# A graph layer's opening: first-hop products in pairs over three slots, the first guess in one piece, list pieces counted anew

## The chip, the cores and the metric

The kernel runs on one core of one Trainium2 chip. The metric is device time in microseconds of one execution, the median of several runs; smaller is better. The profile is one further execution, with its own time.

## The reference

What is computed, cut to what matters (N = 3327 nodes, D = 256, d_attn = 64):

```
h  = relu(layernorm(x))
R  = adj + eye(N);  R = R / R.sum(-1)          # adj is sparse: some five entries a row
Xf = Xa = h;  Z = 0
for n in range(2):
    q = Xa @ W1.T @ W2.T;  k = Xa @ W3.T
    P = softmax(q @ k.T)
    A = P with only the largest entries of each row that make up 0.9 of it
    A = A / A.sum(-1)
    Xf = R @ Xf;  Xa = A @ Xa
    Z += Xf @ U1[n].T + Xa @ U2[n].T
out = x + layernorm(h + Z) * ln_g + ln_b
```

## The kernel before, in words

Rows are cut into NT = 26 tiles of 128. Two steps (n = 0, 1) follow each other, and each walks over the tiles in **slots**: in slot i (from -1 to 27) different tiles are at different stages. The functions named here are generators; each `next` runs them to their next `yield`.

**Stages of a tile in a step.** `weights` (L579) makes the tile's queries, the logits in four chunks (`pl`, two PSUM buffers of two banks in the pool `ps_l`), and their exponentials `e` on ACT. `measured` (L632 in step 0) guesses the threshold of the 0.9 mass: a head of small ACT steps (L617 to L639) and POOL steps (L640 to L643), two passes of ACT over the 3328 entries of each row (relu, then sign; L630), and a tail of small ACT steps (L650 to L656), which ends in five small DVE steps (L659 to L663). `settle` (L719) finds the exact threshold on DVE: `w` (L725, one instruction over 128x3328), 20 MAX8 over segments (`cand`, L730, in two halves), five rounds on the candidates (`bb`, L737 to L749), then the mask of `e` (L759, or in two pieces at L756 for the first and last tile). `Sums` (L792) transposes the masked `e` on PE (`pt`, L805), copies it on ACT (`eT`, L807) and multiplies it with the rows (`pa`, L819). `spread` (L1067) is the sparse product with R: `diffuse` (L902) multiplies gathered adjacency rows `ac` with gathered feature rows `xg` into `pr` (L905). `first_end` (L913) ends a tile of step 0 and, by `prep` (L478), writes next step's keys into the tile `after` and queries into `both`.

**The lists.** `listed` (L832) finds the nonzero columns of each row tile of adj. It loads the tile in pieces and takes the largest of each 128x128 block (`fm`, L841, DVE). The first HALVES = 9 tiles come in two pieces of 832 KB into four spare areas (`roomy`: the scan tile `w`, here called `wide`, and `es[2]`); later tiles come in seven pieces of up to 256 KB into `at` (two buffers). A list ends with some eight small DVE steps (L844 to L852). `packed` and `gathered` (L857, L869) turn a list into indices, load the diagonal block of adj (L883, SP), and issue ten indirect DMAs on POOL: five of adj rows (L888) and five of feature rows (L897), in step 0 from the DRAM table `bx`.

**The products.** Row tile t of h times both matrices of U1 (512 columns) is needed in two DRAM tables before the gathers: `ax[t]` (the part for the end) and `bx[:, t]` (the part to be spread). `products` (L976) makes them: two matmuls into one PSUM bank (`pz`, L982), taken in turn from `ps_r` and `ps_a`, one buffer each; then one copy (L985) into `uh`, four buffers in `es[3]`, on DVE or on ACT; then two DMA writes on SP (L986, L987). A table row that is gathered must have been written, so the first gather of `bx` waits for all 26 tiles.

**What sets the order.** On PE, ACT and DVE the instructions of the two steps stand in the order of the text (L1182 to L1185). That order is written by hand: each slot has seven parts, and a string for each part tells which generators are advanced, one letter for one `next`: m measured, d settle, s spread, w weights, e first_end, a a list piece, p packed, g gathered, b products, q the next tile's queries. `PLAN[0]` is step 0's (L1096). Beside it, two b come at the start of each part in slots -1 and 0 (L1158), and `work` (L1125 to L1138) bounds what a slot may take: list pieces are 3 in slot 0 and otherwise up to 9, of which five letters make five; products are MADE = 13 in slot -1 and the rest in slot 0 (L1152). At the slot's end what is left of the letters at L1174 is run out. POOL in step 0 and SP aren't tied to the text; a scheduler places them, and on each the instructions then run in that fixed order.

**The opening** (L997 to L1054) comes ahead of the slots: a loop over q = 0 to 17 takes pairs of row tiles through the layer norm (bn on DVE, `mv` in two buffers; rstd and scale on POOL, L1010 to L1013; relu on ACT, L1034), transposes (`pt`, L1036), keys and queries (`pk`, L1023; copied to `both` by DVE, L1000) and a Gram matrix (`pgram`, L1041). From q = 5 on one list piece is run in each turn (L1015). Two product tiles are started early by the scheduler, in this loop. After it `moments` (L501) turns the Gram matrix into what the guesses need (`gs`, `qm`), and `project` (L513) makes the first three tiles' laws (`mq`, L529 and L535; `ms` on POOL).

The lines that set the order, as they stand:

```
COUNTED = [t for t in range(NT - 2) if t % 2 == 0]
MADE = 13
HALVES = 9
...
    PLAN = (("mdsssa", "mcdsssa", "edawwp", "msda", "mpdea", "gdwwq", "emgq"),
...
                a=itertools.islice(lister, 9 if i else 3) if step == 0 else none,
...
                for c in "bb" + ({**OPEN, **LAST}.get(i, PLAN[1]) if step else PLAN[0])[k]:
                    next(work[c], None)
```

Of the kernel before, what the change touches and what calls it, by code (L numbers as in the profile page):

```python
# [9 lines left out]
F32 = mybir.dt.float32  # L10
# [8 lines left out]
P = 128  # L19
N = 3327  # L20
D = 256
DA = 64
NT = (N + P - 1) // P
NP = NT * P
ND = D // P
# [298 lines left out]
HALF = NT // 2  # L324
PARTS = -(-NT // 4)
AHEAD = (2, 2)
COUNTED = [t for t in range(NT - 2) if t % 2 == 0]
MADE = 13
HALVES = 9
FIRST = 8 * P  # L330
CUT = 4

# [12 lines left out]
def guess_graph_layer(ctx, tc, x, adj, w1t, w2t, w3t, u1t, u2t, ln_g, ln_b, out, flag):  # L345
    nc = tc.nc
# [8 lines left out]
    small = ctx.enter_context(tc.tile_pool(name="small", bufs=4))  # L355
    ps_l = ctx.enter_context(tc.tile_pool(name="ps_l", bufs=2, space=PSUM))
    ps_t = ctx.enter_context(tc.tile_pool(name="ps_t", bufs=2, space=PSUM))
    ps_a = ctx.enter_context(tc.tile_pool(name="ps_a", bufs=1, space=PSUM))
    ps_r = ctx.enter_context(tc.tile_pool(name="ps_r", bufs=1, space=PSUM))

    V, G, S, PE = nc.vector, nc.gpsimd, nc.scalar, nc.tensor

    rows_of = lambda t: min(P, N - t * P)
    valid = lambda t: 0 <= t < NT
# [8 lines left out]
    after = nodes.tile([P, HALF, P], F32, tag="after", name="after")  # L373
# [24 lines left out]
    u1 = const.tile([P, ND, 2, D], F32, tag="u1", name="u1")  # L398
# [1 line left out]
    gam = const.tile([P, D], F32, tag="gam", name="gam")  # L400
    bet = const.tile([P, D], F32, tag="bet", name="bet")
    uh = es[3][:, : 4 * (2 * D + 1)].rearrange("p (n d) -> p n d", n=4)
    G.memset(uh[:, :, 2 * D :], 1.0)
    for e in (es[0], es[1], es[3]):
        G.memset(e[:, N:NP], 0.0)
    half = const.tile([P, 4], F32, tag="half", name="half")
# [31 lines left out]
    ax = dram.tile([NT, P, D], F32, tag="ax", name="ax")  # L438
    bx = dram.tile([P, NT, D + 1], F32, tag="bx", name="bx")
# [5 lines left out]
    bb = const.tile([P, TOPK + 1], F32, tag="bb", name="bb")  # L445
# [505 lines left out]
    def proof():  # L951
        prove(1)
        yield
        pf = ps_t.tile([P, 4, P], F32, tag="pt", name="pf")
        PE.matmul(pf[:1, 0, :1], fl, ones, start=True, stop=True)
        V.tensor_copy(flag, pf[:1, 0, :1])

    live, ohs, acs, xgs, done, early = {}, {}, {}, {}, [], {}
    none = iter(())
# [14 lines left out]
    hT = xw.rearrange("p t (c r) -> p t c r", r=P)  # L974

    def products():  # L976

        for t in range(NT):
            pool, tag = ((ps_r, "pr"), (ps_a, "pa"))[t % 2]
            pz = pool.tile([P, 2 * D], F32, tag=tag, name="pz")  # L980
            for c in range(ND):
                PE.matmul(pz, hT[:, t, c, :], u1[:, c].rearrange("p n d -> p (n d)"),  # L982
                          start=c == 0, stop=c == ND - 1)
            u = uh[:, t % 4, :]
            (V.tensor_copy if t < MADE and t % 2 or t >= MADE and t % 3 == 0 else S.copy)(u[:, : 2 * D], pz)  # L985
            nc.sync.dma_start(ax[t], u[:, :D])  # L986
            nc.sync.dma_start(bx[:, t, :], u[:, D:])  # L987
            yield

    wide = scan.tile([P, NP], F32, tag="w", name="wide")  # L990
# [2 lines left out]
    lister, product = listed(), products()  # L993
# [3 lines left out]
    for q in range(HALF + 5):  # L997
        if 0 <= q - 3 < HALF:
            k, pk = q - 3, made.pop(q - 3)
            V.tensor_copy(both[:, :, k, :], pk[:, :2, :])  # L1000
            if 2 * k in COUNTED:
                V.tensor_copy(krs[:, k % 2, :DA], pk[:, 2, :DA])
        if q < HALF:
            mv = small.tile([P, 2, 2], F32, tag="mv2", name="mv2", bufs=2)
            rn = small.tile([P, 2, 2], F32, tag="rn2", name="rn2", bufs=3)
            for h in range(2):
                st = small.tile([P, 6], F32, tag="bn", name="st")
                V.bn_stats(st, x0[:, 2 * q + h, :])
                V.bn_aggr(mv[:, h, :], st)
            G.tensor_scalar(rn[:, 0, :], mv[:, :, 1], LN_EPS, None, ALU.add)  # L1010
            G.tensor_tensor(rn[:, 0, :], rn[:, 0, :], half[:, 0::3], ALU.pow)
            G.tensor_tensor(rn[:, 1, :], mv[:, :, 0], rn[:, 0, :], ALU.mult)
            G.tensor_scalar(rn[:, 1, :], rn[:, 1, :], -1.0, None, ALU.mult)  # L1013
            scaled[q] = rn
        if q >= 5:  # L1015
            run(lister, 1)
        if 0 <= q - 2 < HALF:
            k, pt = q - 2, turned.pop(q - 2)
            S.copy(hT[:, 2 * k : 2 * k + 2].rearrange("p t c r -> p (t c) r"), pt)
            pk = ps_t.tile([P, 4, P], F32, tag="pt", name="pk")  # L1020
            for h in range(2):
                for c in range(ND):
                    PE.matmul(pk[:, h, :], wk[:, c, h * DA : h * DA + P], hT[:, 2 * k + h, c, :],  # L1023
                              start=c == 0, stop=c == ND - 1)
            if 2 * k in COUNTED:
                for c in range(ND):
                    PE.matmul(pk[:, 2, :DA], hT[:, 2 * k, c, :], wk[:, c, :DA], start=c == 0, stop=c == ND - 1)
            made[k] = pk
        if 0 <= q - 1 < HALF:
            k, rn = q - 1, scaled.pop(q - 1)  # L1030
            pt = ps_t.tile([P, 4, P], F32, tag="pt", name="pt")
            for h in range(2):
                t = 2 * k + h
                S.activation(x0[:, t, :], x0[:, t, :], AF.Relu, bias=rn[:, 1, h : h + 1], scale=rn[:, 0, h : h + 1])  # L1034
                for c in range(ND):
                    PE.transpose(pt[:, 2 * h + c, :], x0[:, t, c * P : (c + 1) * P], ident)  # L1036
            turned[k] = pt
        if 0 <= q - 4 < HALF and 2 * (q - 4) in COUNTED:
            k = q - 4
            kr = krs[:, k % 2, :]  # L1040
            PE.matmul(pgram[:DA, : DA + 1], kr[:, :DA], kr, start=2 * k == COUNTED[0], stop=2 * k == COUNTED[-1])  # L1041
        if q == 6:
            run(begun[0], 1)
        if q in (8, 11, 14):
            run(begun[0], 1)
        if q in (9, 12):
            run(begun[q // 3 - 2], 1)
        if q == 5:
            for n in range(2):
                nc.sync.dma_start(u1[:, :, n], u1t[n].rearrange("(c p) e -> p c e", p=P))  # L1050
        if q == 10:
            pw = ps_t.tile([P, 4, P], F32, tag="pt", name="pw")
            PE.transpose(pw[:, 0, :], w2d, ident)
            S.copy(w2x, pw[:, 0, :])  # L1054
# [31 lines left out]
    def refetch(t):  # L1086
# [6 lines left out]

    PLAN = (("mdsssa", "mcdsssa", "edawwp", "msda", "mpdea", "gdwwq", "emgq"),  # L1096
            ("llcmss", "lnms", "lwwnfd", "lcmdsssggggg", "fsmwqdf", "llmdf", "lmwd"))

    LAST = {NT - 1: ("cfss", "cn", "nd", "sss", "fdddddsf", "f", ""), NT: ("c", "", "", "ff", "ff", "fv", "f"),
            NT + 1: ("fv", "f", "", "", "f", "f", "f")}  # L1100
    OPEN = {-1: ("llcmss", "lnms", "lwwnfd", "lcmdsssggggg", "fmgswqdf", "llmdf", "lmwfdm"),
            0: ("cmssggg", "nms", "wwnfd", "cmdsss", "fsmgwqdf", "mdf", "mwd"),
            1: ("cmss", "nms", "wwnfd", "cmdsssggggg", "fsmwqdf", "mgdf", "mwd")}
    OPEN[2] = OPEN[3] = OPEN[1]
    fetching = itertools.chain(*(refetch(t) for t in range(NT)))
# [6 lines left out]
    for step in range(2):  # L1112
        sums = Sums(step, live, xw if step else x0, AHEAD[step])

        for i in range(-1, NT + 2):
# [4 lines left out]
            if step == 1 and i == -1:  # L1120
# [9 lines left out]
                s=spread(step, i - 2 + 2 * step) if valid(i - 2 + 2 * step) else none,  # L1130
                w=later.pop((step, i + 2), none),
                e=first_end(i - 2) if step == 0 and valid(i - 2) else none,
                a=itertools.islice(lister, 9 if i else 3) if step == 0 else none,
                p=packed(i + 1) if step == 0 and i >= 0 and valid(i + 1) else none,
                g=fetching if step else gathered(i) if valid(i) else none,
                b=none, q=none, v=proof() if step and i == NT else work.get("v", none),
                l=laws(range(3, NT)) if step and i == -1 else work["l"] if step and i == 0 else none,
            )  # L1138
            if i >= 0 and valid(i + 3):
# [8 lines left out]
                work["w"] = begun[1] if step == 0 else itertools.chain(begun[1], begun[2])  # L1148
            if step == 0 and i == 0:
                work["w"] = begun[2]  # L1150
            if step == 0 and i < 1:
                work["b"] = itertools.islice(product, MADE if i else NT)  # L1152
            for k in range(PARTS):
                g = PARTS * (i - 1) + k - LATE[step]
                summing = valid(g // PARTS)
                if step and valid((g + AHEAD[1]) // PARTS):
                    sums.turn(g + (k == 2), min(i, NT - 1))
                for c in "bb" + ({**OPEN, **LAST}.get(i, PLAN[1]) if step else PLAN[0])[k]:  # L1158
                    next(work[c], None)
                if summing and not step:  # L1160
                    sums.turn(g, min(i, NT - 1))
                for n in BLOCKS[step].get(k, (0,)) if summing else ():
                    ended = sums.sum(g + n)
                    if ended and step == 0:
                        live["r", ended[0]] = ended[1]
                    elif ended:
                        work["f"] = finish(ended[0], live.pop(("f", ended[0])), *ended[1])
# [3 lines left out]
                G.memset(es[2][:, N:NP], 0.0)  # L1171
            if step and i < 1:
                next(fetching)
            for c in ("lcnwqsepb" if i > -1 else "cnwqsepb") if step else "cmwqsepgb":  # L1174
                run(work[c])
            if step == 0 and i == NT:
                moments(1, gsum)
# [52 lines left out]
```

## Time and profile before

| | |
|---|---|
| median of 3 runs | 1404.44 us (1404.25 to 1408.04) |
| the profiled execution: its time | 1405.77 us |
| its span, first to last instruction | 1404.0 us |
| granted TensorE clock, mean | 0.981 |
| end of the loop over q | 53.6 us |
| first w (L725) of step 0: tiles 0, 1, 2 | 86.04, 115.92, 141.07 us |
| later distances from w to w in step 0 | 23.8 to 26.6 us |
| first `pr` of a spread in step 0 | 143.35 us |

How to read it: the page gives for each engine the busy time and share (PE is TensorE's matmuls, PEld its weight loads, DVE VectorE, ACT ScalarE, POOL GpSimd, SP the engine that issues most DMAs; L and a number is a line of the kernel). A row of digits gives busy tenths in 40 equal slices of the span. In a list of waits stand the waiting engine and line, what released it, the total in us, how often, and the longest. In a timeline stand start, length, engine, line, operation, output and input with shapes, count, and in brackets the idle time ahead of it and what ended it. An fp32 matmul shows as two records.

### The profile page before, as it was taken

Reading aid. Unit: us, or ns where it says so; the run is one execution under the profiler, and the core shown is the slowest. Engines: PE = TensorE matmul, PEld = TensorE weight load, DVE = VectorE, ACT = ScalarE, POOL = GpSimd, SP = SyncE. Lnnn points to the kernel's source line nnn. Section 1 sums busy time; section 2 is a strip of 40 time slices with the busy share of each in tenths; the row PEclk is TensorE's granted clock in tenths of the full one; section 3 lists DMA queues with packets and bytes.
Section 4 is the critical chain, followed back from the end, with each engine's and each line's share of the span. In section 5 each row is a group of like instructions: output and inputs, shape, how many; then the busy total and the mean of one; then the engine's idle time right before and its main releaser. Section 6 shows DMA issues by size and latency. Waiting matters only on the chain.

```text
span 1404.0 us, 22095 instructions
## 1 busy us (share of the span) xinstructions
PE 1275.7 (91%) x6495; PEld 976.9 (70%) x6495; DVE 1195.0 (85%) x3673; ACT 1105.3 (79%) x2451; POOL 795.3 (57%) x1243
## 2 busy tenths in 40 slices
PE   6897999999999999999999759999999999999985
PEld 5545777777767777777777537777777777777764
DVE  6878898898988979989882489999998999999993
ACT  5467777878877778778773689999998999999941
POOL 6225766666657656666673475655655555565522
PEclk9999999999999999999999879999999999999998
DMA  8884453444444534534422121322312223132200
GB/s 279 269 269 122 118 145 109 128 138 117 128 125 115 143 107 122 146 111 125 126 78 83 51 72 45 90 77 60 91 56 80 67 70 88 50 89 73 63 20 22
DMA packets 91203, 149.77 MB, mean 107 GB/s; under 512 B 15266, under 2 KB 58657, under 8 KB 91073
## 3 DMA queue, kind: packets, MB, share of 16 engines
q1 hardware_dynamic: 73616, 105.37, 23.8%
q0 software_dynamic: 16640, 42.69, 12.3%
q8 instruction: 54, 0.88, 0.3%
q14 instruction: 77, 0.62, 0.1%
q10 hardware_dynamic: 816, 0.20, 0.1%
HBM read 120.93 MB, written 27.28 MB: 106 GB/s over the span
## 4 chain that ended last, share of the span: by engine, by line
PE 43%; DVE 40%; ACT 11%; issue 4%; DMA 1%; POOL 1%; SPq 0%; another core or an unknown queue 0%; DVEq 0%; ACTq 0%; POOLq 0%
PE pa L819 18%; DVE cand L730 8%; DVE w L725 7%; PE pt L805 6%; DVE e L759 5%; PE pr L905 4%; PE pl L597 4%; DVE cand L739 3%; ACT ja L630 3%; DVE bb L737 3%; PE pz L982 3%; PE pz L918 3%; DVE x L759 2%; ACT eT L807 2%; PE pk L1023 1%
## 5 line engine op out<-in xcount | busy, mean ns | idle before, releaser
L819 PE MATMUL pa<-xw,eT 128*128 128x256 f32 x1352 | 323.6, 384 | 27.4 <-DVE s L929 26.2
L630 ACT ACTIVATE ja<-e,g 128x3328 uint8<-128x3328 f32 x106 | 325.7, 3073 | 0.1
L819 PE MATMUL pa<-x,eT 128*128 128x256 f32 x1352 | 325.2, 382 | 0.0
L819 PEld LDWEIGHTS pa<-xw,eT 128*128 128x128 f32 x1352 | 250.7, 190 | 77.9 <-DVE s L929 31.6
L807 ACT COPY eT<-pt 128x512 f32<-128x512 f32 (+1 forms) x364 | 200.6, 559 | 119.8 <-PE pt L805 100.5
L819 PEld LDWEIGHTS pa<-x,eT 128*128 128x128 f32 x1352 | 244.8, 192 | 26.3
L730 DVE MAX8 cand<-w 128x8 f32<-128x168 f32 (+1 forms) x1040 | 251.4, 317 | 0.0
L805 PE MATMUL pt<-ident,e 128*128 128x128 f32 x1144 | 176.1, 276 | 18.2 <-DVE e L756 9.1
L897 POOL DMA_INDIRECT xg<-bx,index x130 | 156.6, 1205 | 45.2 <-issue 31.5
L805 PEld LDWEIGHTS pt<-ident,e 128*128 128x128 f32 x1144 | 140.9, 144 | 57.7 <-issue 29.2
L725 DVE SCALAR_TENSOR_TENSOR w<-e,g 128x3328 f32<-128x3328 f32 x44 | 162.1, 3684 | 0.7
L888 POOL DMA_INDIRECT ac<-in_adj,index x130 | 130.3, 1002 | 44.5 <-issue 29.6
L897 POOL DMA_INDIRECT xg<-vx,index x130 | 129.5, 996 | 38.6 <-issue 38.6
L759 DVE SCALAR_TENSOR_TENSOR e<-e,rec 128x3328 f32<-128x3328 f32 x40 | 147.5, 3688 | 0.6
L905 PE MATMUL pr<-xg,ac 128*128 128x257 f32 (+1 forms) x520 | 140.6, 395 | 6.8 <-DVE s L1080 6.8
L601 ACT ACTIVATE e<-pl 128x832 f32<-128x832 f32 x132 | 113.8, 867 | 17.9 <-PE pl L597 14.4
L905 PEld LDWEIGHTS pr<-xg,ac 128*128 128x128 f32 x520 | 94.0, 194 | 32.1 <-issue 14.2
L737 DVE MAX8 bb<-cand 128x8 f32<-128x160 f32 x286 | 92.6, 324 | 6.4
L597 PE MATMUL pl<-after,qT 64*128 64x416 f32 x416 | 95.5, 553 | 0.0
L597 PE MATMUL pl<-both,qT 64*128 64x416 f32 x416 | 90.4, 538 | 0.8 <-DVE both L1000 0.8
L673 POOL TENSOR_SCALAR g<-g,law 128x1 f32<-128x1 f32 x23 | 46.4, 2017 | 67.4 <-ACT g L672 67.4
L922 POOL TENSOR_TENSOR sv<-sv,x 128x256 f32<-128x256 f32 x26 | 19.8, 763 | 109.9 <-ACT sv L921 109.9
(255 smaller groups left out, 2153.5 us busy)
## 6 DMA issues: line engine op xcount, KB each, us to landing
at<-in_adj SPq DMA_DIRECT2D x102, 256.0 KB
cx<-ac SPq DMA_DIRECT2D x26, 384.0 KB
ac<-cx SPq DMA_DIRECT2D x26, 384.0 KB
wide<-in_adj SPq DMA_DIRECT2D x10, 832.0 KB
e<-in_adj SPq DMA_DIRECT2D x8, 832.0 KB
bx<-e SPq DMA_DIRECT2D x26, 128.5 KB
own<-bx SPq DMA_DIRECT2D x26, 128.5 KB
x<-in_x SPq DMA_DIRECT2D x13, 256.0 KB
```

Source lines behind the costliest of these rows:

```text
L597: PE.matmul(pl[:, a, :wd], qT[p, :], keys_of(step, a).rearrange("p a b -> p (a b)")[:, c : c + wd], start=True, stop=True)
L630: S.activation(ja, e, f, bias=guess, scale=sign, accum_out=total)
L725: V.scalar_tensor_tensor(w, e, col(16), e, ALU.is_lt, ALU.mult, accum_out=d2)
L730: V.max(cand[:, 8 * s : 8 * s + 8], w[:, s * SEG : min(NP, (s + 1) * SEG)])
L737: V.max(b8, cand)
L759: V.scalar_tensor_tensor(e, e, at(1), e, ALU.is_ge, ALU.mult, accum_out=ra)
L805: PE.transpose(pt[:, j, :], e[:, (j0 + j) * P : (j0 + j + 1) * P], ident)
L807: S.copy(eT[:, :w, :], pt[:, :w, :])
L819: PE.matmul(self.pa, eT[:, c - 4 * k, :], self.xa[:, j, :], start=c == 0, stop=c == NT - 1)
L888: G.indirect_dma_start(out=ac[:, k, :], out_offset=None, in_=rows, in_offset=bass.IndirectOffsetOnAxis(ap=index[:, t, k : k + 1], axis=0), ...
L897: G.indirect_dma_start(out=xg[:, k, :w], out_offset=None, in_=rows, in_offset=bass.IndirectOffsetOnAxis(ap=index[:, t, k : k + 1], axis=0))
L905: PE.matmul(pr[:, :w], ac[:, k, :], own if k == KT - 1 else xg[:, k, :w], start=k == 0, stop=k == KT - 1)
```

## The change

- `products` works on 13 pairs of tiles. Even pairs go into the two banks of `ps_r` and `ps_a`; odd pairs, and the last, into one two-bank buffer of the pool `ps_l`, which the logits use too. A pair takes two letters b: one for its four matmuls, one for its two copies and four writes. Copies are DVE's for the first four pairs and for odd ones, else ACT's.
- The copies of the last four tiles go into `uk`, three buffers in the tile `after`.
- Slots -1, 0 and 1 of step 0 get strings of their own (`BEGIN`), with 7, 12 and 7 letters b: 8, 12 and 6 tiles are multiplied in them. The two b ahead of each part go. In slot -1 relu and sign passes of tile 0's guess are advanced in one part, and the chunks of tile 1's logits come in parts 2 and 3 (before: 2 and 5).
- The gathers of tile 0 are begun in slot 0 and run out in part 3 of slot 1, after the last b.
- Lists: HALVES is 7, so 14 pieces are big and 133 small (18 and 119 before). The loop over q runs 10 pieces instead of 13; slots -1 and 0 run 4 and 6 (before 5 and 3), slot 1 and later odd slots 6, even ones 5 (before 5 each); part 5 of `PLAN[0]` gets the sixth a.
- `mv` has four buffers instead of two.

```diff
-MADE = 13
-HALVES = 9
+HALVES = 7
...
-    G.memset(uh[:, :, 2 * D :], 1.0)
+    uk = after.rearrange("p j r -> p (j r)")[:, : 3 * (2 * D + 1)].rearrange("p (n d) -> p n d", n=3)
+    for u in (uh, uk):
+        G.memset(u[:, :, 2 * D :], 1.0)
...
-        for t in range(NT):
-            pool, tag = ((ps_r, "pr"), (ps_a, "pa"))[t % 2]
-            pz = pool.tile([P, 2 * D], F32, tag=tag, name="pz")
-            for c in range(ND):
-                PE.matmul(pz, hT[:, t, c, :], u1[:, c].rearrange("p n d -> p (n d)"),
-                          start=c == 0, stop=c == ND - 1)
-            u = uh[:, t % 4, :]
-            (V.tensor_copy if t < MADE and t % 2 or t >= MADE and t % 3 == 0 else S.copy)(u[:, : 2 * D], pz)
-            nc.sync.dma_start(ax[t], u[:, :D])
-            nc.sync.dma_start(bx[:, t, :], u[:, D:])
+        for s in range(HALF):
+            if s % 2 or s == HALF - 1:
+                pl = ps_l.tile([P, 2, 512], F32, tag="pl", name="pz")
+                pzs = [pl[:, h, :] for h in range(2)]
+            else:
+                pzs = [ps_r.tile([P, 2 * D], F32, tag="pr", name="pz"), ps_a.tile([P, 2 * D], F32, tag="pa", name="pz")]
+            for h in range(2):
+                for c in range(ND):
+                    PE.matmul(pzs[h], hT[:, 2 * s + h, c, :], u1[:, c].rearrange("p n d -> p (n d)"),
+                              start=c == 0, stop=c == ND - 1)
+            yield
+            for h, pz in enumerate(pzs):
+                t = 2 * s + h
+                u = uh[:, t % 4, :] if t < NT - 4 else uk[:, t % 3, :]
+                (V.tensor_copy if s < 4 or s % 2 else S.copy)(u[:, : 2 * D], pz)
+                nc.sync.dma_start(ax[t], u[:, :D])
+                nc.sync.dma_start(bx[:, t, :], u[:, D:])
             yield
...
-            mv = small.tile([P, 2, 2], F32, tag="mv2", name="mv2", bufs=2)
+            mv = small.tile([P, 2, 2], F32, tag="mv2", name="mv2", bufs=4)
...
-        if q >= 5:
+        if 5 <= q < 15:
             run(lister, 1)
...
-    PLAN = (("mdsssa", "mcdsssa", "edawwp", "msda", "mpdea", "gdwwq", "emgq"),
+    PLAN = (("mdsssa", "mcdsssa", "edawwp", "msda", "mpdea", "gdawwq", "emgq"),
...
+    BEGIN = {-1: ("mba", "mmbba", "mwwbbaa", "bmwwb", "", "", ""),
+             0: ("mdbba", "mcdbba", "medbwwbap", "mdabb", "mpdbwwba", "gdabbq", "q"),
+             1: ("mdsssbba", "mcdsssbba", "edbawwbp", "msdbga", "mpdea", "dawwq", "emgq")}
...
-                a=itertools.islice(lister, 9 if i else 3) if step == 0 else none,
+                a=itertools.islice(lister, 5 + i % 2 if i > 0 else 6) if step == 0 else none,
...
-                g=fetching if step else gathered(i) if valid(i) else none,
-                b=none, q=none, v=proof() if step and i == NT else work.get("v", none),
+                g=fetching if step else itertools.chain(work.get("g", none), gathered(i)) if valid(i) else none,
+                b=none if step else product, q=none, v=proof() if step and i == NT else work.get("v", none),
...
-            if step == 0 and i < 1:
-                work["b"] = itertools.islice(product, MADE if i else NT)
...
-                for c in "bb" + ({**OPEN, **LAST}.get(i, PLAN[1]) if step else PLAN[0])[k]:
+                for c in ({**OPEN, **LAST} if step else BEGIN).get(i, PLAN[step])[k]:
...
-            for c in ("lcnwqsepb" if i > -1 else "cnwqsepb") if step else "cmwqsepgb":
+            for c in ("lcnwqsepb" if i > -1 else "cnwqsepb") if step else "cmwqsep" + "gb" * (i > 0):
```

## The prediction

> **What bounds the kernel now.** First the page: PE is the busiest engine and the chain that ended last is 43% PE, 40% DVE. The row of 40 slices (35.1 us each) shows where PE is not full in the first half: at the very start, and in the second (35 to 70 us, 8) and fourth (105 to 140, 7).
>
> ```profile
> PE 1275.7 (91%) x6495; PEld 976.9 (70%) x6495; DVE 1195.0 (85%) x3673; ACT 1105.3 (79%) x2451; POOL 795.3 (57%) x1243
> ...
> PE   6897999999999999999999759999999999999985
> ```
>
> The change lies wholly in the opening and slots -1 to 2 of step 0, with list pieces up to slot 23. So I cut that stretch by the busy time of the engines. Columns: length, then PE, PEld, DVE, ACT, POOL busy, granted clock, DMA share, GB/s.
>
> ```profile
> 17.17:53.60 36.43, 36.06 (x231) 28.59 (x231) 28.95 (x79) 17.40 (x36) 13.33 (x34) 1.00 0.84 287
> ...
> 114.00:119.30 5.30, 1.04 (x9) 0.80 (x7) 5.16 (x14) 4.90 (x12) 2.85 (x2) 1.00 0.14 50
> 119.30:126.10 6.80, 5.12 (x14) 3.79 (x16) 6.73 (x28) 2.69 (x5) 5.32 (x12) 0.50 0.40 128
> ```
> ```profile
> 53.60:143.35 89.75, 75.60 (x259) 39.82 (x257) 72.92 (x211) 59.26 (x139) 37.02 (x60) 0.96 0.64 200
> ```
>
> The loop over q runs at PE's speed (36.06 of 36.43). From its end to 143.35, where PE meets the first spread matmul `pr` of tile 0, PE idles 89.75 - 75.60 = 14.15 us, and 5.12 us of its work falls at half clock, which costs 2.6. So 16.7 us are to be had there, no more. Who holds PE:
>
> ```profile
> PE pt L805 <- ACT eT L807: 5.9, 1, 5.9
> PE pz L982 <- ACT e L985: 2.6, 1, 2.6
> PE po L873 <- ACT eT L807: 1.4, 1, 1.4
> PE pz L982 <- DVE e L985: 1.4, 1, 1.4
> PE pq L506 <- DVE lists L847: 1.1, 1, 1.1
> ```
>
> The longest is slot 1's start: PE's products are used up, and the first `eT` copy stands on ACT behind tile 2's guess and a 3.05 us pass.
>
> ```profile
> 112.71 1.45 PE L982 MATMUL pz<-u,xw 128*128 128x512 f32 x3
> 114.00 1.04 PE L805 MATMUL pt<-ident,e 128*128 128x128 f32 x8
> 120.98 1.12 PE L805 MATMUL pt<-ident,e 128*128 128x128 f32 x4 [5.94 <-ACT eT L807]
> 121.89 3.62 PE L819 MATMUL pa<-x,eT 128*128 128x256 f32 x8
> ```
>
> **Prices.** A product tile is 4 records of 0.4375 (24 in 10.50), so 1.75; a pair 3.5. A logits chunk 0.8, its exponential 0.84. A pass L630 3.07 + 0.19; the guess's head L619-L639 2.4, its tail L650-L656 2.5. A product copy 0.6. A big list reduce 1.88, a small one 0.6, a list's ending 1.3. Settling: w 3.68, each half of cand 2.4, bb and cum 4.3, mask 3.7 to 3.9. I walk the order in which the changed kernel's instructions stand on each engine, with these durations, on the clock of the profiled execution.
>
> **The opening.** With four `mv` buffers instead of two, DVE no longer waits for POOL, but POOL's order changes too: it now takes the scale of q = 0, 1, 2 in one batch, so the first rstd waits for the third tile pair.
>
> ```profile
> 7.47 1.64 DVE L1008 BATCH_NORM_STATS2 st<-x 128x6 f32<-128x256 f32 x4 [1.57 <-DMA x<-in_x]
> ...
> 8.24 2.07 ACT L1034 ACTIVATE x<-x,rn 128x256 f32<-128x256 f32 x4 [6.16 <-DVE st L1008]
> ...
> 17.17 0.48 PE L1041 MATMUL pgram<-krs 128*64 128x65 f32 x2 [2.66 <-DVE krs L1002]
> ```
>
> The third mv is there at 9.0; three powers of 0.7 and the small steps give the first scale at 12.1, where ACT started at 8.24: 3.9 later. Of that PE's wait of 2.66 before `pgram` hides most: q = 0's products are then done at 17.4, DVE reaches the copy of `both` after its bn work at 18.2, `pgram` at 18.9, 1.7 later than 17.17. Those lines ran at the half-clock start, so warm it is 0.9. Bounds: -1 (nothing lost, and DVE's early copies help) and +3.9 (all of it). I take +0.9, the walk.
>
> **The end of the loop and slot -1.** Three big reduces (5.6 us of DVE) and their 832 KB loads leave this stretch, so gs comes right after the last copy of `both`: `pq` at 54.6 instead of 56.72, the first step of the guess that needs the law (L619) at 59.4 instead of 63.63. With relu and sign next to each other the guess of tile 0 ends at 70.7; it ended at 81.93. DVE can start w at 71.5 instead of 86.04. PE gains less: pair 1 sits in the `pl` pool, so the logits of tile 1 wait for its DVE copies, which stand behind a big reduce (1.8 idle), and the third chunk waits for tile 1's exponentials, now behind both passes (68.7 to 71.6: 2.9 idle). With 0.9 at the loop's end and 0.4 in small waits, PE ends pair 3 at 76.9; with as much done it stood at about 78 before.
>
> **Slot 0.** Twelve tiles 21.0, four chunks 3.2, small things: 25 us, no wait over 0.1, since each copy has a part of slack and pairs alternate. DVE's 6.7 us of waits for `pz` (L985, five times) go; three more small reduces (1.8) and two more copies come. It ends the mask of tile 0 at 98.2 and starts tile 1's w at 99.3 (115.92 before), with mask 1 at 119.9 (133.88 before).
>
> **Slot 1.** Pair 11 ends at 109.5, pair 12 fills PE from 114.2. The old hole of 5.94 and its 2.6 of half clock are covered by 10.5 us of products. eT comes at 110.6, before PE asks. PE reaches `pr` of tile 0 at 131.6 by the walk. If I take instead PE's own work, 75.60 - 2.6 = 73.0, plus the 6.6 of idle that I counted (0.9, 1.8, 2.9, 0.4, and 0.6 at an eT), it is 133.2. The handovers that the walk leaves out are in the second; I take 133.
>
> **What is late next.** The gathers of tile 0 read the whole of bx, so they wait for pair 12. Its copies are on ACT until 123.4, and its four writes stand on SP behind three list loads and the cx write; the last of those loads waits for a DVE reduce at 119.9, so ACT decides: bx is complete near 126. Five gathers follow, 1.25 apart (124.27, 125.66, 126.93 ...), landing about 2.7 after their start (an estimate from the packets of that queue). But w of tile 2 runs from 128 to 131.7, and then POOL stands:
>
> ```profile
> 85.92 0.97 POOL L888 DMA_INDIRECT ac<-in_adj,index  x1 [0.30 <-issue]
> 87.19 3.35 POOL L888 DMA_INDIRECT ac<-in_adj,index  x1 [0.30 <-issue]
> ```
>
> The second met w at 86.04 to 89.7 and ended 0.85 after it. The Trainium skill (SBUF — State Buffer, "SBUF: two separate sides") says that DVE and GpSimd take one port pair as an exclusive lock, and that a DMA issued by GpSimd then starves for descriptors. This speaks against putting the gathers here. Free of it, the third has landed at 131.3 and the fifth at 133.8, and PE waits for nothing. With it the third starts after w, ends at 132.6 and lands at 134.2, the fifth at 136.7, and PE's two groups of `pr` wait 1.2 and 0.5. I take 1.7, as the row of POOL shows the block; bounds 0 and 5. POOL's guess work for tile 3 comes after eleven gathers, near 146, and L650, which came 19.6 after w (135.56 after 115.92), needs it near 148: hidden, by 2.
>
> Sum at `pr`: 133 + 0.9 + 1.7 = 135.6 against 143.35, so -7.7. A gap under one 3.4 us window leaves the clock alone: the same skill (TensorE: Matmul & The Clock Gate, "The HAM clock gate") sets that as the least, the trace has 2.6 without and 5.9 with a half clock; my 2.9 lies nearer the first. Each such fall would cost 2.6.
>
> **Later slots.** Lists: 11 more small reduces and two more endings in slots 1 to 23, 11 x 0.6 + 2 x 1.3 = 9.2 us of DVE. They stand after the mask, where DVE idles up to 1.9 before L535 each slot. Bounds: -1.5 (DVE comes 4 us ahead into slot 2, slots near 214 to 240 hung on it) and +9.2. I take +0.5, as the chain there is nearly all PE. The change is therefore -7.2: the profiled execution's 1405.77 (span 1404.0) would be 1398.6, and from the median of 1404.44, which lies 1.3 below it, it is 1397.2.
>
> **Rivals.** *All goes well*: no start delay, gathers before w: 0.9 + 1.7 + 1 of the handovers more, 1393.6. For it: PE's first wait of 2.66. Against: the batch on POOL. *The cover is thin*: both PE waits (2.9, and 1.7 at `pr`) grow past a clock window, 2 x 2.6 = 5.2, so 1402.4; or half of the list pieces shows, 4.6 less the 0.5 taken, 1401.3. I take 1402. For it: PE's order has no other work there. Against: the slot periods were set by PE. *Slower*: gathers late. If DVE does not run ahead and mask 1 stays at 133.9, the list load frees SP only then, bx is complete at 137.5, w at 141.07 to 144.7 holds POOL after three gathers, the fifth lands at 149.6, and `pr`, which before ended at 147.2, ends at 150.7; half clock adds 2.6: +6, 1410.5. It decides from the moment when that reduce comes later than 129 or so; by 119.9 in the walk it doesn't.
>
> **Chances.** Likeliest 0.50 (1397.2, its own 1394.5 to 1400.5), all well 0.22 (1393.6), thin cover 0.17 (1402), slower 0.11 (1410.5). The range 1391 to 1403.5 leaves out the slower case and the outer tails. About 0.3% (4.2 us) can be told from no change. Faster by more: 0.46 of the likeliest, 0.22, and 0.06 of thin cover, 0.74; within: 0.15; slower: 0.11.
>
> **What would show it.** Right: ACT's first L1034 near 12; w of tile 0 near 72 and of tile 1 near 99; no `pt` wait for eT over 1 us near 110 and no half clock there; `pr` of tile 0 near 136 with waits for gathers of about 1.7; slot periods of 25 to 26 after. Wrong: w of tile 0 after 80 (the guess isn't what held it), a half-clock row near 70 or 133, or slot periods up by 0.4.

## The result, and the profile after

On the chip of the first traces the changed kernel takes 1402.97 us (median of 20 runs, 1395.44 to 1409.54) against 1404.74 of the kernel before (20 runs): ratio 0.9986, 95% interval 0.9974 to 0.9998. The forecast was -7.2 us; -1.8 came, a quarter of it, and only just clear of no change. The profiled execution took 1402.92 us, with a span of 1401.2. Three other chips run the kernel before in 1365 us; on the one of them where the changed kernel ran, too (6 runs), it is slower: 1.0070 (1.0052 to 1.0087). Both have to be explained.

The page after, its row of engines and PE's row of 40 slices (35.0 us each):

```profile
PE 1276.6 (91%) x6495; PEld 976.5 (70%) x6495; DVE 1199.8 (86%) x3689; ACT 1102.5 (79%) x2445; POOL 814.9 (58%) x1244
...
PE   5898899999999999999999769999999999999985
```

The dip in the fourth slice is shallower (8 instead of 7), and the first, third and fifth are each a tenth lower. The same by stretches, cut where the forecast cut it (length, then PE, PEld, DVE, ACT, POOL busy, clock, DMA share, GB/s): from the end of the loop to the first `pr`, on to the z products of tile 0 (L919, the first product of the result of tile 0), and the eight us in slot -1 that a clock fall covers.

```profile
53.60:138.78 85.18, 76.83 (x257) 39.05 (x258) 69.52 (x198) 56.84 (x134) 23.27 (x47) 0.96 0.52 161
138.78:158.48 19.70, 14.96 (x69) 11.43 (x68) 12.08 (x50) 10.97 (x19) 15.41 (x23) 0.91 0.53 145
```
```profile
65.00:73.00 8.00, 7.23 (x12) 2.87 (x12) 6.13 (x13) 7.05 (x14) 3.93 (x6) 0.57 0.92 296
```

PE meets the first `pr` at 138.78, 4.6 us earlier than before. But from there to the z products it takes 19.70, where the kernel before took 12.59 without idling:

```profile
143.35:155.94 12.59, 12.59 (x69) 10.28 (x68) 12.28 (x43) 11.62 (x20) 10.14 (x16) 1.00 0.55 154
```

So the z products come 2.5 us later (158.48 against 155.94), and the loss lies behind the first `pr`.

PE's waits from 53.6 to 159 (total, times, longest):

```profile
PE pr L906 <- DMA xg<-bx,index: 3.6, 2, 3.0
PE pl L598 <- DVE e L993: 3.5, 2, 2.8
PE pl L598 <- ACT e L602: 2.2, 2, 1.1
PE pt L806 <- ACT xT L475: 1.1, 1, 1.1
...
PE pt L806 <- ACT eT L808: 0.2, 1, 0.2
```

The wait of 5.9 for eT is down to 0.2, as forecast. In its place stand waits for the logits buffers (3.5 and 2.2) and for gathers (3.6). Their total, 13.8 with those not shown, is nearly what PE idled before (14.1).

Where it went is told by four sections of the trace, since the end of the loop differs by up to 4 us from one trace to another. A is the last `pgram` (end of the loop). *Stretch* is from A to the z products of tile 0, with the same matmuls in every kernel; *from `pr`* is the part of it behind the first `pr`. *Slots* goes on to the last w of step 0, *rest* to the end of the span. PE idle is the stretch less its records; half clock is the time in the stretch at a granted clock of 0.5. The times of a row are of one execution; its ratio is of all runs, to the kernel before on the same chip, in turns.

| kernel | A | stretch | from `pr` | PE idle | half clock | slots | rest | ratio (95%) |
|---|---|---|---|---|---|---|---|---|
| before, first chip | 52.4 | 103.5 | 12.6 | 14.1 | 6.8 | 571.5 | 676.5 | |
| after, first chip | 51.5 | 107.0 | 19.7 | 13.8 | 10.2 | 565.2 | 677.5 | 0.9986 (0.9974-0.9998) |
| r_before | 52.8 | 100.2 | 12.6 | 10.8 | 10.2 | 537.4 | 674.7 | |
| r_after | 50.9 | 104.3 | 17.2 | 11.7 | 10.2 | 541.0 | 676.4 | 1.0070 (1.0052-1.0087) |
| t_sp | 54.3 | 104.8 | 17.7 | 12.3 | 10.2 | 540.3 | 675.4 | 1.0062 (1.0047-1.0076) |
| t_copy | 53.7 | 100.3 | 15.0 | 12.1 | 0 | 539.2 | 675.7 | 1.0075 (1.0063-1.0088) |
| t_both | 53.6 | 100.3 | 14.1 | 8.9 | 6.8 | 542.4 | 675.4 | 1.0051 (1.0039-1.0063) |
| t_gap | 53.4 | 103.5 | 17.2 | 12.6 | 6.8 | 540.9 | 676.4 | 1.0070 (1.0043-1.0097) |
| a_pass | 54.2 | 107.7 | 19.8 | 13.5 | 13.7 | 540.3 | 673.9 | 1.0080 (1.0065-1.0095) |
| x_two | 52.6 | 104.9 | 12.6 | 13.1 | 13.7 | 538.1 | 675.9 | 1.0061 (1.0039-1.0083) |
| l_old | 51.0 | 109.2 | 18.3 | 16.9 | 10.2 | 538.4 | 674.5 | 1.0066 (1.0049-1.0083) |
| n_single | 52.3 | 111.2 | 19.9 | 17.4 | 17.1 | 535.8 | 677.3 | 1.0096 (1.0082-1.0110) |
| b_lists | 51.7 | 95.8 | 12.6 | 8.2 | 6.8 | 539.9 | 676.0 | 1.0005 (0.9995-1.0016) |
| b_guess | 50.2 | 98.3 | 12.6 | 9.8 | 6.8 | 539.5 | 674.9 | 1.0012 (1.0003-1.0021) |
| t_only | 52.8 | 100.5 | 12.6 | 10.1 | 6.8 | 537.4 | 674.5 | 1.0007 (0.9996-1.0018) |
| n_turn | 53.6 | 96.5 | 12.6 | 7.4 | 6.8 | 537.2 | 675.4 | 0.9982 (0.9976-0.9989) |

So the opening lost, on both kinds of chip: the stretch is 3.5 and 4.1 us longer, not some 8 shorter. The slots behind it give 6.3 back on the first chip and cost 3.6 on the other. The part from `pr` is 12.6 in all seven kernels with products over two slots, and 14.1 to 19.9 in all nine with three.

### The profile page after: what moved, and what is told of

The parts are those of the page before. It is cut to its first block, busy times and chain, and to the rows that moved or that the text cites. A ratio compares the mean times of both kernels' runs of the same rounds, so it can differ in the third digit from the quotient of the medians.

```text
span 1401.2 us, 22108 instructions
## 1 busy us (share of the span) xinstructions
PE 1276.6 (91%) x6495; PEld 976.5 (70%) x6495; DVE 1199.8 (86%) x3689; ACT 1102.5 (79%) x2445; POOL 814.9 (58%) x1244
## 3 DMA queue, kind: packets, MB, share of 16 engines
q0 software_dynamic: 16640, 42.69, 12.3%
## 4 chain that ended last, share of the span: by engine, by line
DVE 43%; PE 41%; ACT 9%; issue 5%; POOL 1%; DMA 1%; SPq 0%; DVEq 0%; POOLq 0%; ACTq 0%
PE pa L820 17%; DVE cand L731 9%; DVE w L726 8%; PE pt L806 5%; DVE e L760 5%; PE pl L598 4%; PE pr L906 4%; DVE cand L740 4%; DVE bb L738 3%; PE pz L919 3%; ACT ja L631 3%; DVE x L760 2%; PE pz L987 2%; ACT eT L808 1%; DVE fm L842 1%
## 5 line engine op out<-in xcount | busy, mean ns | idle before, releaser
L898 POOL DMA_INDIRECT xg<-bx,index x130 | 165.0, 1269 | 52.0 <-issue 41.6
L889 POOL DMA_INDIRECT ac<-in_adj,index x130 | 142.8, 1099 | 43.9 <-issue 29.1
L842 DVE TENSOR_REDUCE fm<-at 128x4 f32<-128x512 f32 (+1 forms) x133 | 84.5, 635 | 12.8 <-DMA at<-in_adj 11.8
```

The costliest lines, as they stand in the source:

```text
L889: G.indirect_dma_start(out=ac[:, k, :], out_offset=None, in_=rows, in_offset=bass.IndirectOffsetOnAxis(ap=index[:, t, k : k + 1], axis=0), ...
L898: G.indirect_dma_start(out=xg[:, k, :w], out_offset=None, in_=rows, in_offset=bass.IndirectOffsetOnAxis(ap=index[:, t, k : k + 1], axis=0))
```

## The experiments

The first theory was this. By w of tile 2 the changed kernel leads by 5.0 us (136.0 against 141.1) and one slot later it is 0.7 behind (166.9 against 166.2). In between SP stands at the cx write of tile 1, which waits for tile 1's gathers, with the list loads behind it, and DVE waits for the load (SP's queue and DVE, changed kernel):

```profile
132.78 0.33 SPq L841 DMA_DIRECT2D at<-in_adj  x1
149.01 0.32 SPq L1084 DMA_DIRECT2D cx<-ac  x1
149.43 0.38 SPq L841 DMA_DIRECT2D at<-in_adj  x1
```
```profile
154.29 0.69 DVE L842 TENSOR_REDUCE fm<-at 128x4 f32<-128x512 f32 x1 [7.11 <-DMA at<-in_adj]
```

Against this *queue theory* stood the *PE theory*: only PE's gaps and its half clock count, and DVE's lead or wait is cover.

**t_sp.** One dependency added, which puts the cx write of tile 1 behind the next two list loads (cut; `loads` holds the list loads in order):

```
+BEHIND = {1: 29}
...
+            wr = nc.sync.dma_start(cx[t], a.rearrange("p k r -> p (k r)"))
+            if t in BEHIND:
+                tc.add_manual_dep(wr.ins, loads[BEHIND[t]].ins.name, IN_ORDER, reason="order of the text")
```

> The changed kernel with one order on SP's queue: the cx write of tile 1 is issued after the next two list loads instead of ahead of them. Queue theory (the gain of 5.0 us at the third w is given back because SP stands at that write until 149.0 and DVE then waits 7.1 us for a list load at 154.3): the DVE wait goes, the fourth w of step 0 comes at 160 to 162 instead of 166.9, and the kernel takes 1397 to 1399. PE theory (PE was late anyway: it waits 2.8 us for a logits buffer in slot -1 and 3.6 us for gathers at 142, each with a stretch of half clock behind it, and starts tile 0's z products at 158.5, 2.6 later than before): the DVE wait goes too, the fourth w comes earlier, but PE's z products of tile 0 stay at 157.5 to 158.5 and the time at 1401.5 to 1403.

The DVE wait went, from 7.11 (5.45 in r_after) to 0.70 at the same place:

```profile
154.28 0.69 DVE L845 TENSOR_REDUCE fm<-at 128x4 f32<-128x512 f32 x1 [0.70 <-DMA at<-in_adj]
```

But the fourth w came only 1.1 us earlier than in r_after, counted from A (112.4 against 113.5), less than either theory had: DVE now waits 4.9 us for `mq` from ACT. The z products stayed (159.1, a stretch of 104.8 against 104.3) and so did the time, 1.0062. The gain that the queue theory promised didn't come; t_both, where the fourth w does come early, is the harder test of it.

**t_copy.** `"msdbga"` in `BEGIN[1]` becomes `"bmsdga"`.

> The changed kernel with one letter moved: the two ACT copies of pair 12 come ahead of the 3.1 us guess pass in part 3 of slot 1 instead of behind it. Queue theory: bx is complete near 129 instead of 134, the gathers of tile 0 start then and not at 135.0, PE's waits at pr go, but DVE's wait for the list load in slot 2 stays over 4 us, and the time falls by 1 to 2 (1401 to 1402). PE theory: PE loses neither the 3.6 us nor the half clock behind it, the z products of tile 0 start at 153 to 155 instead of 158.5, and the time falls by 3 to 5 (1398 to 1400).

bx came sooner: counted from A, the gathers of tile 0 start at 78.9, against 83.0 in r_after, and PE idles 2.0 instead of 2.7 behind the first `pr`. The stretch is 100.3, 4.0 less than r_after. But this trace has no clock fall, and the one in slot -1 alone is worth 3.1 us (below), so most of the 4.0 isn't the letter's. It is also the fastest of the six runs (1370.6; the others 1374.6 to 1378.3). The time is 1.0075: nothing.

**t_both.** Both edits, and the cx write of tile 0 behind the last bx write.

> Both together, and the cx write of tile 0 behind the last product write: queue theory 1395 to 1397 (the waits in slot 2 are one chain, both have to go); PE theory 1398 to 1400, as with the copies alone. The forecast's own walk would come out here: third w near 134, pr of tile 0 near 135, fourth w near 159.

Stretch 100.3, PE idle 8.9, and the fourth w 5.6 earlier than in r_after after the A's are taken off (107.9 against 113.5). Of the time 0.2% came back (1.0051), with intervals that overlap. Neither theory's number, but 5.6 us of lead on DVE bought next to nothing, and with that the queue theory falls. The clock fall of this trace (58.0, for 6.8 us) stands behind no PE gap of 1 us.

**r_before, r_after.** The two kernels as they are. All three kernels above had run on chips where the kernel before takes 1365 us.

> The kernel before, once more, for its trace: the three kernels made from the changed one ran on a chip on which the kernel before takes 1365 instead of 1404 us (a later slot of step 0 has 24.2 us there, 25.5 in the first traces), and were 0.5 to 0.75% slower than it. Shown if this is again that chip: span near 1364, first w of step 0 at 84 to 86, z products of tile 0 near 148 (156 in the first trace). On the first chip: span near 1403.

> The changed kernel, once more, beside the kernel before. Queue theory and PE theory alike put the loss into slots -1 to 2, ahead of the z products of tile 0, which the variants reached at 153.8 to 159.1. On the chip with slots of 24.2 us nothing later gives it back, so: ratio 1.006 to 1.010 there, z products of tile 0 near 158. On a chip with slots of 25.5: 0.997 to 1.000.

As expected for that chip. From here on everything is compared there.

**x_two.** `BEGIN`: 13 letters b in slot -1, 13 in slot 0, none in slot 1; the gathers of tile 0 at the head of slot 1.

> The changed kernel with its products over two slots again: 13 letters b each in slots -1 and 0, none in slot 1, the gathers of tile 0 at the start of slot 1; pairs, four buffers, the guess of tile 0 and the lists as changed. Queue theory (the third slot makes bx late and crowds the gathers of tiles 0 and 1 into one stretch): bx complete near 115, pr of tile 0 without a wait, z products of tile 0 at 147 to 150 and 0.5 to 0.8% faster than the changed kernel, so about as the kernel before. PE theory (the work on PE is the same, only its gaps count, and slot 1 loses the products that cover the first eT): z products at 152 to 156, within 0.3% of the changed kernel.

`pr` has no wait, as the queue theory has it. But the z products come at 157.5, later than either theory said: the hole at eT is back (5.5), and pairs wait for the exponentials of a logits buffer (3.7). The time is within 0.1% of the changed kernel, as the PE theory has it. So the third slot moved the wait and no more: counted from A, the first `pr` comes 5.2 us earlier with it (87.0 against 92.3), and from `pr` to the z products it takes 4.6 longer. Over two slots or three, the pairs lose.

**t_gap.** `"mmbba", "mwwbbaa"` in `BEGIN[-1]` become `"mmbb", "mbwwbaaa"`.

> The changed kernel with slot -1's letters moved so that pair 1 is copied ahead of the logits chunks of tile 1, which wait for its buffer, and one list piece a part later. PE theory: the wait of 2.83 us at 63 and the stretch of half clock behind it (some 3.2 us) go, and the time falls by 3 to 5 against the changed kernel. Queue theory: the wait goes, first w of step 0 as before at 75, third w 2 earlier at most, the stall in slot 2 takes it: 0 to -1.5.

The wait of 2.8 fell to 0.48, and 3.50 us came at the next chunk, behind the exponentials on ACT, with a clock fall behind it. No gain (1.0070). The gap only moved by one chunk.

**b_lists.** The list counts alone, in the kernel before (HALVES 7, ten pieces in the loop, `islice(lister, 5 + i % 2 if i > 0 else 4 if i else 6)`, `"gdawwq"`).

> The kernel before with only the lists counted anew (HALVES 7, ten pieces in the loop, 4 and 6 in slots -1 and 0, 6 and 5 after, with the sixth letter a). The forecast priced this part in the later slots at +0.5 and the earlier end of the loop's reduces at a gain of first w. If the lists alone explain the later slots, where the changed kernel regains 4.7 us between the fourth w and the end of step 0: 1400 or below. If they cost: 1406 to 1408. If neither: 1404 to 1405, with the first w of step 0 some 3 to 6 us before 86.0.

The stretch is 4.4 us shorter than in r_before (95.8 against 100.2): DVE reaches `gs` earlier, `pq` no longer waits for a list (1.1), the products' wait of 2.6 for an ACT copy is gone, and the clock fall behind that wait with it. The time is the same: what the opening gains is paid behind it, 2.5 us in the slots and 1.3 in the rest.

**l_old.** The complement: the changed kernel with HALVES 9, `q >= 5`, `islice(lister, 9 if i else 3)` and the letters a that go with it.

> The changed kernel with its lists counted as before (HALVES 9: 18 big pieces, 13 of them in the loop, 5 in slot -1, 3 small ones in slot 0, then 5 in a slot). If the 14 more small pieces are what costs behind the opening: from the z products of tile 0 to the last w of step 0 it takes 537 to 538 us as in the kernel before (540.9 in the changed one), the opening loses 2 to 5 of what the earlier end of the guess gave, and the ratio stays at 1.006 to 1.010. If the pieces cost nothing there and only the opening counts: 540 to 542, ratio 1.009 to 1.013.

First branch. The stretch is 4.9 longer than in r_after (PE waits 6.5 us for a logits buffer in slot -1 instead of 2.8), slots and rest together 4.5 shorter, the time the same. Behind the z products it is DVE's mask that PE waits for, here and then in r_after, to the last w of step 0:

```profile
PE pt L806 <- DVE e L760: 3.8, 6, 1.5
```
```profile
PE pt L806 <- DVE e L760: 7.9, 11, 1.2
```

So these two pairs of traces agree on the lists' two sides: -4.4 and -4.9 in the opening, +3.8 and +4.5 behind it. A third pair (t_only, below) has the gain but hardly the cost.

**b_guess.** b_lists, with slot -1's letters `"ma", "mma", "mawwp", "ma", "a", "aww", ""`: the guess in one piece.

> The kernel before with the new list counts and, as one more part of the change, the guess of tile 0 in one piece in slot -1 (relu and sign pass next to each other); products singly, over two slots. PE theory (what ends last is PE; from the loop's last pgram to the z products of tile 0 it took 95.8 us with the lists alone, 100.2 in the kernel before, 104.3 changed): both passes on ACT hold the exponentials of tile 1 and with them the logits buffers, PE waits some 3 us in slot -1, with or without 3 us of half clock behind it, and the stretch is 98 to 102, the time 1.000 to 1.005 of before. Forecast's reading (an early first w is worth something): first w 4 to 5 earlier than with the lists alone (75), stretch 93 to 96, 0.997 to 1.000.

Stretch +2.5 against b_lists. First w is at 80.2, 29.9 behind A, against 28.3 in b_lists: not even earlier. The expected wait for logits didn't come; two product buffers wait for ACT copies instead (2.1). A loss too small to tell (1.0012 against 1.0005).

**a_pass.** The changed kernel with slot -1 as `"mba", "mbba", "wwbbaa", "mbb", "m", "ww", "m"`.

> The changed kernel with the guess of tile 0 in pieces again, as before (and tile 1's last logits chunks in part 5 of slot -1): pairs, four buffers, three slots and lists as changed. If the guess in one piece is what costs: the waits of 2.8 and 1.1 us and the half clock in slot -1 go, stretch from last pgram to z products 98 to 100 instead of 104.3, ratio 1.001 to 1.004. If the pairs and the third slot cost: stretch 102 to 105, ratio 1.005 to 1.008; first w 5 us later either way.

Second branch, and past its stretch: 107.7, 1.0080. In slot -1 PE still waits 3.0 us, for exponentials, with half clock behind it. Both branches had the first w 5 us later; it is not (23.4 behind A against 23.2). The guess in one piece isn't what costs.

**n_single.** Products singly, 13, 9 and 4 in slots -1, 0 and 1, the last four in two buffers of `ps_l`, copied by DVE.

> The change's cover without its pairs: lists as changed, guess in pieces, products singly through two buffers with 13 tiles in slot -1, 9 in slot 0 and the last 4 in slot 1, on both sides of the first pt. If work for PE at the start of slot 1 is what the hole of 5.9 us needs: stretch 88 to 92. If the eT copy is what it needs (it stands on ACT behind tile 2's guess and pass, and PE now arrives there earlier): the hole only moves, stretch 95 to 99.

Worst of all (111.2, past both branches). The product in slot 1 waits for a DVE copy (7.4 in two waits, the longest 6.6) and `pr` for gathers (4.1). Work put into slot 1 to cover a hole brings its own waits, without pairs too.

**n_turn.** b_lists, and ahead of the letters of a part:

```
+                if step == 0 and i == 1 and k == 0:
+                    sums.turn(0, 1)
```

> The kernel before with the new list counts and one call moved: the first transposes of tile 0 and their eT copies come at the start of slot 1, ahead of tile 2's guess and pass on ACT, instead of behind them. Products as before. If ACT's order makes the hole: PE's wait of 5.9 us at eT falls under 1, no half clock at 112, stretch 88 to 91 (95.8 with the lists alone), 0.994 to 0.996 of before. If the hole is owed to something later on DVE or ACT that slot 1 and 2 wait for anyway: 94 to 96 and 0.999 to 1.001.

PE at slot 1's start, with the lists alone and then in n_turn:

```profile
108.53 1.04 PE L805 MATMUL pt<-ident,e 128*128 128x128 f32 x8
115.51 1.12 PE L805 MATMUL pt<-ident,e 128*128 128x128 f32 x4 [5.94 <-ACT eT L807]
```
```profile
110.50 1.04 PE L805 MATMUL pt<-ident,e 128*128 128x128 f32 x8
111.82 0.66 PE L805 MATMUL pt<-ident,e 128*128 128x128 f32 x4 [0.29 <-ACT eT L807]
...
120.55 0.66 PE L805 MATMUL pt<-ident,e 128*128 128x128 f32 x4 [2.21 <-ACT lists L863]
```

The hole closes, and a wait of 2.21 and one of 3.2 at a later `pq` open: PE idle falls by 0.8 only, and the stretch is not shorter. So ACT's order made the hole. Behind it PE meets what is left of ACT's work: the first of the two waits stands behind tile 2's pass of 3.05 and two exponentials, the second behind the tail of its guess, in which ACT itself waits 2.7 us for POOL. The time, 0.9982 (0.9976 to 0.9989), is the best of all here.

**t_only.** The same two lines in the kernel before.

> The kernel before with the moved transposes and eT copies alone, lists as before. With the new list counts beside it this gave 0.9982. If the move is worth its 3 to 5 us by itself: stretch from last pgram to z products 95 to 97 (100.2 before), ratio 0.995 to 0.998. If it only pays because the lists end earlier: 99 to 101, ratio 0.999 to 1.001.

100.5 and 1.0007: it pays only with the lists beside it. With them (n_turn) the stretch is 4.0 shorter, and slots and rest together are only 0.7 longer: that is where the 0.9982 stands in these traces. Why the lists cost so little there isn't shown.

## Why the prediction was wrong

The stretch is where it failed. By its own terms the forecast had PE idle 14.15 falling to 8.3 (6.6 and 1.7), half clock down by 2.6, and the start +0.9, so -7.6 at the first `pr` (it has -7.7, by rounding 133.2 to 133), and nothing behind it. Measured on the first chip: -4.6 at the first `pr`, and then +7.1 from there to the z products, together +2.5. The same by terms: idle 14.1 to 13.8, PE's busy time for the same matmuls 89.4 to 93.2, A 0.9 earlier. Of the 3.8 of busy time 2.4 are half clock (PE was busy at it for 9.9 us instead of 5.1); the other 1.4 isn't explained. So two terms failed: idle of PE that was to go and only moved, and a clock that was to fall no more and fell twice. Step by step:

- *What bounds it, 16.7 to be had*: borne out. In t_both the fourth w came 5.6 us earlier, and the time moved by 0.2%.
- *The opening, +0.9*: first scale at 11.1 (12.1 forecast), `pgram` at 18.64 (18.9). A is at 52.8 on average in ten traces with four `mv` buffers, and at 52.3 in six with two, from 50.2 to 54.3: of the forecast's size, but below the scatter, and no run has the buffers alone.
- *The guess ends earlier*: right in direction. w of tile 0 came at 75.0 (71.5 forecast, 86.0 before), of tile 1 at 107.4 (99.3). Ahead of the first, DVE's pair copies waited 2.1 us for PE; between the two, DVE waited 3.5 for ACT's guess and 2.7 for ACT's `mq`. But an early w was worth nothing here: r_after has its first w 12.7 us earlier than r_before and its z products 2.1 later.
- *Slot -1, idle of 1.8 and 2.9, no half clock*: failed. The first wait, for a `pl` buffer, was 2.83 instead of 1.8, and the clock fell with it; the second came as 0.4. PE in slot -1, changed kernel, then the same opening in t_copy:

```profile
65.77 1.75 PE L598 MATMUL pl<-both,qT 64*128 64x416 f32 x4 [2.83 <-DVE e L993]
67.45 6.06 PE L987 MATMUL pz<-u,xw 128*128 128x512 f32 x8
```
```profile
67.94 0.97 PE L598 MATMUL pl<-both,qT 64*128 64x416 f32 x4 [2.82 <-DVE e L993]
68.84 3.70 PE L987 MATMUL pz<-u,xw 128*128 128x512 f32 x8
```

  The gap is the same to 0.01 us; one execution pays (1.75 - 0.97) + (6.06 - 3.70) = 3.1 us and the other nothing. The granted clock from 65 to 73 is 0.57 in the one. I had taken a gap under one window of 3.4 as safe, from the Trainium skill (TensorE: Matmul & The Clock Gate, "The HAM clock gate"), which gives one idle window as the least for a fall and calls the window free-running, and from one gap of 2.59 in the trace before. The measurement decides: of the 19 PE gaps of 2.6 to 3.5 us between 40 and 175 us in the sixteen traces, 17 have a fall that begins in the gap or up to 1.6 us behind it. The two without are that 2.59 and the 2.82 of t_copy.
- *Slot 1, "what is late next"*: failed. bx was to be complete near 126. Pair 12's copies stood on ACT behind a pass of 3.07 until 129.96, and its last write was issued at 131.4. So the gathers began one us before w of tile 2, which started at 136.04, and the second met it (POOL):

```profile
134.99 0.96 POOL L898 DMA_INDIRECT xg<-bx,index  x1 [9.16 <-issue]
136.26 4.28 POOL L898 DMA_INDIRECT xg<-bx,index  x1 [0.30 <-issue]
```

  w ran for 3.68. The block that the forecast weighed is there (4.28 instead of 0.95), one gather earlier than it had it, and all of it some 8 us later. PE's waits at `pr` were 3.04 and 0.61 instead of 1.7 in all, and the clock fell again (0.91 over 138.78 to 158.48).
- *Slot 0, "no wait over 0.1"*: failed. There, too, logits waited for the buffer of a pair or a pair for that of the logits: 0.65 and 1.05 in slot 0, 1.11 and 0.71 in slot 1.
- *Pairs in `ps_l`, priced at the 1.8 and 2.9 alone*: the term that was too small. The traces can be put into a row with one part of the change more at each step: r_before 100.2, lists 95.8 (b_lists), guess in one piece 98.3 (b_guess), pairs 104.9 (x_two), third slot 104.3 (r_after). The pairs are the +6.6, and the step at which the time goes up: 1.0012 (1.0003 to 1.0021) to 1.0061 (1.0039 to 1.0083). A pair that holds a logits buffer makes two kinds of work wait for each other's copies. That step also brings the four `mv` buffers, `uk`, other copy engines and other places of the letters, which no run takes apart; and 2.2 of the 6.6 are half clock.
- *Later slots, +0.5*: mis-sized. In two pairs of traces out of three the 14 more small pieces cost 3.8 and 4.5 us on the chips where PE is full; on the first chip no run has them alone. From 260 to 500 us, in the order before and after on the first chip, r_before, r_after:

```profile
260.00:500.00 240.00, 225.93 (x1182) 174.09 (x1181) 209.82 (x648) 188.03 (x473) 154.47 (x215) 1.00 0.44 124
```
```profile
260.00:500.00 240.00, 228.07 (x1201) 176.85 (x1200) 217.18 (x662) 189.96 (x480) 163.37 (x217) 1.00 0.46 131
```
```profile
260.00:500.00 240.00, 239.00 (x1275) 189.73 (x1274) 228.74 (x702) 203.04 (x502) 196.66 (x234) 1.00 0.47 135
```
```profile
260.00:500.00 240.00, 235.56 (x1249) 186.29 (x1248) 225.98 (x701) 200.14 (x491) 194.52 (x231) 1.00 0.48 136
```

  On the first chip PE idles 14.1 of 240 before, 11.9 after, so nothing shows of the pieces there. On the other it idles 1.0 before and 4.4 after. My argument that "DVE idles up to 1.9 before L535 each slot" was read from the first chip and held only there: in the slots DVE waits 37 us before L535 in that trace, and not once in r_before.
- *The rivals*: "thin cover" came nearest to the mechanism, PE waits with clock falls behind them, though no wait grew past a window. Its 1402 is the measured time by luck: the z products came some 10 us later than the forecast's terms give, not 5.2, and the slots gave 6.3 back. The slower rival's late gathers came, and cost PE 3.6 at `pr`. That the change ends 0.7% slower on another chip was in no rival.

What stays open: why the first chip gave 6.3 back in the slots. The last section describes where it stands, without a cause.

## What to carry to other kernels

Where one engine sets the pace, count its gaps after the change one by one, also behind the point that the forecast aims at, and charge each of the longer ones a clock fall (here 17 of 19 gaps of 2.6 to 3.5 us had one), instead of counting how far the others run ahead; lead on DVE was worth nothing here. Cover that shares a buffer pool with the work it is to cover, or stands in an ACT or DVE queue behind a long pass, brings back as several short waits what it removed as one long one. And work that looks hidden in idle time of one profile is hidden only while that idle time is there: look whether it is the kernel's own or the chip's.

## What the hardware showed unexpectedly

The same kernel takes 1404.7 us on one chip and 1365.3 on others, at a mean granted clock of 0.98 on both. Most of the difference lies in the slots of step 0 (571.5 against 537.4). ACT, first chip, kernel before; then the same place in r_before:

```profile
255.70 3.10 ACT L630 ACTIVATE ja<-e,g 128x3328 uint8<-128x3328 f32 x1
258.68 0.22 ACT L630 ACTIVATION_READ_ACCUMULATOR ja<-e,g 128x1 f32 x1
261.93 0.59 ACT L807 COPY eT<-pt 128x512 f32<-128x512 f32 x1 [3.03 <-PE pt L805]
```
```profile
247.46 3.10 ACT L630 ACTIVATE ja<-e,g 128x3328 uint8<-128x3328 f32 x1
250.44 0.22 ACT L630 ACTIVATION_READ_ACCUMULATOR ja<-e,g 128x1 f32 x1
250.53 0.60 ACT L807 COPY eT<-pt 128x512 f32<-128x512 f32 x1
```

The transposes named as releaser (PE, 256.52, 0.60 long) were done 4.8 us before the copy began. In 22 slots ACT stands like this, 67.5 us in all; in the changed kernel, first chip, 15 times at this copy and 4 times at L920, 55.9 us. PE's waits for `eT` at `pq`, from the z products to the last w of step 0, fall from 29.8 to 24.4 us, which is most of the 6.3 that came back. That fewer stands made them fall is argued, not shown. In r_before and r_after ACT does not stand behind this pass. No view names a cause, and no later run fell on the first chip, so neither the stand nor its part in the result was tried.

Half clock followed gaps of PE well under the 3.4 us that I had counted on. Of the four traces with the same gap of 2.8 us in slot -1, three (2.83, 2.81 and 2.83) went to half clock for 6.8 us and one (2.82) did not. Of the 34 gaps of 1.0 to 2.2 us in the same part of the sixteen traces none has a fall of its own; a fall lasted 3.4 or 6.8 us, and 10.2 once.
